# A conditioned feed-forward with routed low-rank experts: the chosen heads of two tiles turned by copies and VectorE instead of by TensorE, and deltas that follow later

## The chip, the cores and the metric

The kernel runs on one core of one Trainium2 chip. The metric is the device time of one execution in microseconds, as the median of several runs. A profile is one further execution, taken with the hardware profiler; its own time is given beside its span, because durations come from it.

## What is computed

The inputs are x (8 batches of 512 tokens, 2048 columns, float32), a base matrix W (2048 x 2048) with a bias, 32 low-rank adapters of rank 16 of which each batch uses one (`itok`), a router for 8 experts, and for each expert a projection A to 16 columns and a matrix B back to 2048. Cut to what matters:

```python
def cond(x, slot, W, b, As, Bs):                # x: (b t i)
    base = einsum('bti,oi->bto', x, W) + b
    return base + 2.0 * ((x @ As[slot]) @ Bs[slot])

def ffn(y, route_w, A, Bw):
    logits = einsum('bsd,ed->bse', y, route_w)  # 8 logits
    value, index = top_k(logits, 1)
    weight = one_hot(index, 8) * value
    h = einsum('bsd,erd->bser', y, A)           # 8 x 16 heads
    return einsum('bser,eor->bso', weight[..., None] * h, Bw)

out = x + ffn(cond(x, itok, ...), ...)
```

Nothing stands between the two parts but matrix products, so the kernel folds router and A (136 columns: 128 heads and 8 scores) into W and the adapters once for each batch, and multiplies x by the 2048 x 136 result.

## The kernel before

**Stages.** First W is read in 16 row blocks and folded with the projection (`fold_w`, L293), together with the adapters of the first batch. Then a loop runs over 32 tiles of 128 tokens. A pair of tiles is a unit; x is kept in five buffers of one unit each. `Q` is 32, `NQ` is 4.

**One tile.** The heads are `x_tile @ m`, with x turned so that its columns lie on partitions. The turn has two steps: `shuffle` (L249) copies 16 blocks of 32 partitions for a whole unit, some on ScalarE and some on GpSimd, so that each block of 32 x 32 lies where its transpose belongs; `turn_x` (L234) transposes blocks of 32 x 32 on VectorE (DVE). TensorE then multiplies 16 column blocks into a PSUM tile `ph` of 128 x 136 (`heads`, L452). `route` (L463 to L473) is the choice, six DVE instructions: add the constant part, take the greatest score, find its first place, and set all heads but the chosen 16 to zero, scaled by the score (`wh`). `turn_heads` (L520) transposes `wh` on TensorE into PSUM (`pw`), and `keep_heads` (L525) copies the result to SBUF on ScalarE (`whT`). `delta` (L558) multiplies `whT` by the experts' B (`fb`) in halves of 1024 columns (two matmuls of 512) into PSUM (`po`). `add_delta` (L571) adds such a half to x on DVE, and behind the second half `store` (L580) writes the tile out from the SP queue.

**Order.** The order of all engines is written out by hand (`manual_schedule`); each engine runs its instructions in the order in which the code issues them. The loop at L606 counts half tiles, n. In one n TensorE has 8 matmuls of heads, then a half delta. The half delta of n is that of half tile n - 3 (`piece`), its addition comes one n later, and the transposed heads stand at the end of even n. ScalarE and GpSimd have 4 shuffles in each n, for the unit that TensorE reaches some six n later.

**Folding an adapter.** For each batch but the first, `fold_adapter` (L481) makes the batch's matrix m in the n that `folded` lists (5, 11, 19, 27, 35, 43, 51): small products on TensorE (L349), copies on ScalarE (L504, L510), additions on DVE (L508), and three n later additions on GpSimd (`add_c`, L512). It uses both `po` buffers, so that n has no delta and the next n has two.

**PSUM.** There are 8 banks: `ps_s` and `ps_h` two tiles of one bank each, `ps_o` two tiles of two banks. `ph` of tile 0 lies in `ps_s`, that of the others in `ps_h`; `pw` and two products of a fold lie in `ps_s`.

**Loads.** `load_x` (L118) reads a unit into the buffer of the unit five before it, from the SP queue. It is issued five n behind the delta of that older unit's last half (L643), and has to wait until that unit is copied away and stored.

**The end.** For the last two tiles `ends` lists PSUM banks piece by piece; each piece of 512 or 256 columns is added and stored by itself, some of the last tile's from ScalarE's queue.

Of the kernel before, what the change touches and what calls it, by code (L numbers as in the profile page):

```python
# [9 lines left out]
F32 = mybir.dt.float32  # L10
# [8 lines left out]
def kernel(  # L19
# [33 lines left out]
    P = 128  # L53
# [24 lines left out]
    small = ctx.enter_context(tc.tile_pool(name="small", bufs=2))  # L78
    wctx = ctx.enter_context(ExitStack())
    wpool = wctx.enter_context(tc.tile_pool(name="wpool", bufs=1))  # L80
    ps_s = ctx.enter_context(tc.tile_pool(name="ps_s", bufs=2, space=bass.MemoryType.PSUM))
    ps_c = wctx.enter_context(tc.tile_pool(name="ps_c", bufs=1, space=bass.MemoryType.PSUM))

    ctx.enter_context(tc.manual_schedule())
# [43 lines left out]

    nc.scalar.copy(warm_a[:, 1:2], warm_a[:, :1])
    load_pj(1, 3, nc.scalar)  # L130
    pm = ps_s.tile([P, P], F32, tag="s", name="pm")
    for _ in range(12):
        nc.tensor.matmul(pm, warm, warm, start=True, stop=True)

    own_i = const.tile([P, B], I32, name="own_i")
    nc.gpsimd.iota(own_i, pattern=[[-R, B]], base=0, channel_multiplier=1)
# [105 lines left out]
    def shuffle(u, ms, copy):  # L242

        if not ms:
            return
        if u not in xq_tiles:
            xq_tiles[u] = qpool.tile([P, TPU, NQ, DQ], F32, tag="q", name=f"xq_{u}")
        for g, i in ms:
            copy(xq_tiles[u][ts(i, Q), :, g, :], x_tiles[u][ts(g, Q), :, ts(i, DQ)])  # L249
# [71 lines left out]
            copy(bq[ts(i, Q), g].rearrange("p (c a) -> p c a", a=Q), src[:, :, i, :])  # L321

    def project_bias():
        pb = ps_s.tile([P, NP], F32, tag="s", name="pb")
        nc.tensor.matmul(pb, warm, bp, start=True, stop=True)
        nc.vector.tensor_copy(c0b, pb)

    pg = ps_s.tile([P, NP], F32, tag="s", name="pg")

    def project_adapters():  # L330

# [90 lines left out]
                turn_x(0, h)  # L422
    first_products()
    wctx.close()
    ps_h = ctx.enter_context(tc.tile_pool(name="ps_h", bufs=2, space=bass.MemoryType.PSUM))
    ps_o = ctx.enter_context(tc.tile_pool(name="ps_o", bufs=2, space=bass.MemoryType.PSUM))
    xpool2 = ctx.enter_context(tc.tile_pool(name="xpool2", bufs=1))
    ms[1] = [xpool2.tile([P, n, NP], F32, name=f"m1_{n}") for n in parts]
    xpools.update({k: xpool2 for k in range(3, XB)})


    ph_tiles = {}
    wh_tiles = {}
    pw_tiles = {}
    whT_tiles = {}
    po_tiles = {}

    def batch_of(t):
        return t // TPB

    def place_heads(t):
        if t not in ph_tiles:

            pool, tag = (ps_h, "h") if t else (ps_s, "s")
            ph_tiles[t] = pool.tile([P, 512], F32, tag=tag, name=f"ph_{t}")

    def heads(t, j0, j1):
        if j0 == 0:
            place_heads(t)
        m = ms[batch_of(t) % 2]  # L450
        for j in range(j0, j1):
            nc.tensor.matmul(  # L452
                ph_tiles[t][:, :NP],
                xT_tiles[t][:, j, :],
                place(m, (j,))[:, 0, :],
                start=(j == 0),
                stop=(j == NJ - 1),
            )

    def route(t):  # L460

        ph = ph_tiles[t][:, :NP]
        nc.vector.tensor_tensor(ph, ph, c0b, ALU.add)  # L463
        top = small.tile([P, 1], F32, tag="top", name=f"top_{t}")
        nc.vector.tensor_reduce(top, ph[:, ER:NP], AX.X, ALU.max)
        key = ph_tiles.pop(t)[:, NP : NP + E]
        nc.vector.scalar_tensor_tensor(key, ph[:, ER:NP], top, rank, ALU.is_equal, ALU.mult)
        win = small.tile([P, 1], F32, tag="win", name=f"win_{t}")
        nc.vector.tensor_reduce(win, key, AX.X, ALU.max)
        rw = small.tile([P, E], F32, tag="rw", name=f"rw_{t}")  # L470
        nc.vector.tensor_scalar(rw, key, win, top, ALU.is_equal, ALU.mult)  # L471
        wh = small.tile([P, ER], F32, tag="wh", name=f"wh_{t}")
        nc.vector.tensor_tensor(  # L473
            wh.rearrange("p (e r) -> p e r", r=R),
            ph[:, :ER].rearrange("p (e r) -> p e r", r=R),
            rw.unsqueeze(2).to_broadcast([P, E, R]),
            ALU.mult,
        )
        wh_tiles[t] = wh

    def fold_adapter(b, t):  # L481

        place_heads(t + 1)
        lasts = [
            ps_s.tile([P, 512], F32, tag="s", name=f"pa_{b}_{k}")[:, :NP] for k in range(2)
        ] + [ph_tiles[t + k][:, ds(NP + E, NP)] for k in range(2)]
        banks = []  # L490
        for k in range(2):
            po = ps_o.tile([P, HN, 512], F32, tag="o", name=f"po_{b}_{k}")
            banks += [
                po[:, n, : GRP * NP].rearrange("p (j e) -> p j e", e=NP) for n in range(HN)
            ]

        for q in reversed(range(NQ)):
            adapter_product(b, lasts[q], q, 3)
        for n in range(3):
# [12 lines left out]
    def add_c(b):  # L512
# [2 lines left out]
            nc.gpsimd.tensor_tensor(place(m, js), place(m, js), place(cs, js), ALU.add)  # L515
        nc.gpsimd.tensor_tensor(m[1], m[1], cs[1], ALU.add)

    def turn_heads(t):
        pw = ps_s.tile([P, P], F32, tag="s", name=f"pw_{t}")
        nc.tensor.transpose(pw, wh_tiles.pop(t), ident)  # L520
        pw_tiles[t] = pw

    def keep_heads(t):
        whT_tiles[t] = small.tile([P, P], F32, tag="whT", name=f"whT_{t}")
        nc.scalar.copy(whT_tiles[t], pw_tiles.pop(t))  # L525

    def bank(tag, n):

        pool, shape = {
            "h": (ps_h, [P, 512]), "s": (ps_s, [P, 512]), "o": (ps_o, [P, HN, 512])  # L530
        }[tag]
        b = pool.tile(shape, F32, tag=tag, name=f"pe_{tag}")
        return n, (b[:, 0, :] if tag == "o" else b)[:, :n]


    ends = {
        (NT - 2, 0): (("o", 512), ("o", 512)),
        (NT - 2, 1): (("h", 512), ("s", 512)),
        (NT - 1, 0): (("h", 512), ("o", 512)),
        (NT - 1, 1): (("o", 512), ("h", 256), ("s", 256)),  # L540
    }

    def delta(t, h, within=None):

        c0 = h * D // 2
        if (t, h) in ends:
            cuts = ends[t, h]
        else:
            po = ps_o.tile([P, HN, 512], F32, tag="o", name=f"po_{t}_{h}")
            cuts = [(512, po[:, k, :]) for k in range(HN)]  # L550
            po_tiles[t, h] = [(ds(c0, D // 2), po.rearrange("p n d -> p (n d)"))]
        c = c0
        for cut in cuts:
            if (t, h) in ends:
                cut = bank(*cut)
                po_tiles.setdefault((t, h), []).append((ds(c, cut[0]), cut[1]))
            n, part = cut
            nc.tensor.matmul(part, whT_tiles[t], fb[:, ds(c, n)], start=True, stop=True)  # L558
            c += n
            if within:  # L560
                within()
                within = None

    def add_delta(t, h, n=None):

        u, k = divmod(t, TPU)
        pieces = po_tiles[t, h]
        po_tiles[t, h] = pieces[n:] if n else []
        for m, (cols, part) in enumerate(pieces[:n]):
            xs = x_tiles[u][:, k, cols]  # L570
            nc.vector.tensor_tensor(xs, xs, part, ALU.add)  # L571
            if (t, h) in ends:
                store(t, cols, nc.scalar if t == NT - 1 and m % 2 else nc.sync)
            elif h == 1:
                store(t, ds(0, D))

    def store(t, cols, eng=nc.sync):
        u, k = divmod(t, TPU)
        b, r = divmod(t, TPB)
        eng.dma_start(out=out[b, ts(r, P), cols], in_=x_tiles[u][:, k, cols])  # L580

    def piece(n):

        return divmod(n - 3, 2) if 0 <= n - 3 < 2 * NT else (-1, -1)

    def shuffle_slot(n):

# [11 lines left out]
        shuffle(*shuffle_slot(n), nc.gpsimd.tensor_copy)  # L599


    folded = {8 * b + (3 if b else 5): b + 1 for b in range(B - 1)}
    folds = folded.get
    adds_c = {8 * b + (5 if b else 6): b + 1 for b in range(B - 1)}.get

    for n in range(2 * NT + 4):  # L606
        t, h = divmod(n, 2)
        if t < NT:
            heads(t, h * HJ, h * HJ + HJ // 2)
            if n == 3:  # L610

                turn_heads(0)
            heads(t, h * HJ + HJ // 2, (h + 1) * HJ)
        tp, hp = piece(n - 1)
        if tp >= 0 and not folds(n - 1):
            add_delta(tp, hp)
        turn_x(t + 1, h)
        if h == 1 and 0 < t <= NT:
            keep_heads(t - 1)
        if folds(n):  # L620
            fold_adapter(folds(n), t)
        if h == 1 and t < NT:
            route(t)
        u, ms_u = shuffle_slot(n)
        shuffle(u, ms_u, nc.gpsimd.tensor_copy if n == 2 else nc.scalar.copy)
        if adds_c(n):
            add_c(adds_c(n))
        if folds(n):
            pass
        elif n == 2 * NT:  # L630

            delta(*piece(n), lambda: turn_heads(t - 1))
        else:
            if folds(n - 1):
                delta(*piece(n - 1))
                add_delta(*piece(n - 1))
            if piece(n)[0] >= 0:
                delta(*piece(n))
            if n == 2 * NT - 1:
                add_delta(*piece(n), 1)  # L640
        if h == 0 and 1 < t < NT:
            turn_heads(t - 1)
        tq, hq = piece(n - 5)  # L643
        u, k = divmod(tq, TPU)
        if tq >= 0 and hq == 1 and k == TPU - 1 and u + XB < NU:
            load_x(u + XB)


# [46 lines left out]
```

## Time and profile before

| what | value |
|---|---|
| median of 3 runs | 319.52 us (319.36 to 319.61) |
| the profiled execution's own time | 319.83 us |
| its span (first to last instruction) | 318.1 us |
| granted TensorE clock | 0.998 |
| busy: TensorE, DVE, ScalarE, GpSimd | 312.0, 237.7, 188.0, 163.0 us |
| matmuls of the heads (L452), of the deltas in `po` (L558), of W (L293): busy | 129.8, 111.7, 59.9 us |
| transposes of `wh` on TensorE (L520) | 32 |
| moved by DMA | 88.5 MB, 278 GB/s in the mean |
| longest wait: ScalarE's copy `whT` for `pw` | 56.4 us in 25 waits |
| GpSimd's shuffles for x to land | 32.8 us in 7 waits |
| a store of 1 MB, issue to landing | 4.9 us median, 3.9 from 285 us on |

Busy time is the time in which an engine had at least one instruction at work. In the lists of groups each line has source line, engine, operation, tile written and tile read, shape, count, busy time, mean of one in ns, and the idle time before it with what ended it. The chain is followed back from the last instruction, at each step to what released it. `PEld` is the loading of weights, which lies beside the matmuls. A matmul in float32 appears as two records.

### The profile page before, as it was taken

To read this page: it belongs to the slowest core of one execution; us is meant where nothing else is said; L and a number is where in the kernel's file an instruction comes from. 1 tells how busy PE (TensorE), PEld (TensorE's weight loads), DVE (VectorE), ACT (ScalarE), POOL (GpSimd) and SP (SyncE) were. 2 spreads that over 40 slices of the span, in tenths; PEclk is the share of its full clock that TensorE was granted. 3 is DMA by queue.
4 is the path that set the end of the run, shared out by engine and by line. 5 is a ranking of instruction groups with operands and counts; after the bars stand their busy time and mean duration, and the time that the engine had idled before them with its cause. 6 is when DMAs were issued, how large, how long until landed. Compare 5 with 4: busy or idle time off the path is not lost.

```text
span 318.1 us, 5569 instructions
## 1 busy us (share of the span) xinstructions
PE 312.0 (98%) x2140; PEld 246.9 (78%) x2140; DVE 237.7 (75%) x422; ACT 188.0 (59%) x245; POOL 163.0 (51%) x167
## 2 busy tenths in 40 slices
PE   8999999999999999999999999999999999999994
PEld 7999999999777777786777767777777777677762
DVE  2231788947888798878887987887888888888864
ACT  3332466748697497659765965677587749760000
POOL 1012085989994949094819553935396276710000
PEclk9999999999999999999999999999999999999999
DMA  7999999989323494959495858767685859444337
GB/s 276 413 363 415 422 422 418 418 315 388 143 117 158 173 362 169 384 199 374 160 395 178 364 174 354 249 280 247 282 317 213 322 236 364 168 168 169 162 149 249
DMA packets 15307, 88.52 MB, mean 278 GB/s; under 512 B 1696, under 2 KB 4016, under 8 KB 4912
## 3 DMA queue, kind: packets, MB, share of 16 engines
q1 hardware_dynamic: 14112, 85.45, 68.6%
q0 software_dynamic: 320, 2.11, 1.6%
q10 hardware_dynamic: 848, 0.61, 0.6%
q8 instruction: 17, 0.28, 0.4%
q14 instruction: 10, 0.08, 0.1%
HBM read 54.60 MB, written 33.55 MB: 277 GB/s over the span
## 4 chain that ended last, share of the span: by engine, by line
PE 96%; DMA 2%; DVE 1%; DVEq 0%; issue 0%
PE ph L452 38%; PE po L558 32%; PE pc L293 19%; DMA w<-in_w_dram 2%; PE po L349 2%; PE pg L333 1%; PE pw L520 1%; PE pe_o L558 1%; PE ph L349 1%; PE pe_h L558 1%; DVE x L571 0%; PE pc L349 0%; PE pe_s L558 0%; DVE m L370 0%; DVE wv L279 0%; DVEq L691 0%
## 5 line engine op out<-in xcount | busy, mean ns | idle before, releaser
L249 POOL COPY xq<-x 32x1024 f32<-32x1024 f32 x121 | 126.0, 1041 | 77.8 <-DMA x<-in_x_dram 32.8
L249 ACT COPY xq<-x 32x1024 f32<-32x1024 f32 x135 | 140.9, 1043 | 15.3 <-DMA x<-in_x_dram 13.3
L452 PEld LDWEIGHTS ph<-m,xT 128*128 128x128 f32 x1024 | 124.8, 190 | 21.1 <-issue 15.8
L452 PE MATMUL ph<-m,xT 128*128 128x136 f32 x1024 | 129.8, 280 | 0.3 <-DVE m L370 0.3
L558 PE MATMUL po<-fb,whT 128*128 128x512 f32 x240 | 111.7, 592 | 0.0
L571 DVE TENSOR_TENSOR x<-x,po 128x1024 f32<-128x1024 f32 x60 | 72.9, 1217 | 28.5 <-PE po L558 28.3
L234 DVE STREAM_TRANSPOSE xT<-xq 128x1024 f32<-128x1024 f32 x64 | 78.8, 1235 | 2.0 <-POOL xq L249 1.4
L558 PEld LDWEIGHTS po<-fb,whT 128*128 128x128 f32 x240 | 41.7, 190 | 32.0 <-issue 31.8
L293 PE MATMUL pc<-pj,wv 128*128 128x136 f32 x512 | 59.9, 280 | 0.3 <-DVE wv L279 0.3
L293 PEld LDWEIGHTS pc<-pj,wv 128*128 128x128 f32 x512 | 59.5, 190 | 0.5 <-DVE wv L279 0.5
L525 ACT COPY whT<-pw 128x128 f32<-128x128 f32 x32 | 8.5, 265 | 56.5 <-PE pw L520 56.4
L279 ACT COPY wv<-w 128x1024 f32<-128x1024 f32 (+1 forms) x17 | 16.8, 996 | 30.2 <-DMA w<-in_w_dram 28.5
L279 DVE COPY wv<-w 128x1024 f32<-128x1024 f32 (+1 forms) x17 | 11.6, 685 | 25.5 <-DMA w<-in_w_dram 14.9
L515 POOL TENSOR_TENSOR m<-m,c 128x408 f32<-128x408 f32 x14 | 14.4, 1048 | 1.6 <-ACT m L510 1.1
L221 POOL COPY ad_q<-ad_ar 32x512 f32<-32x512 f32 x12 | 9.3, 773 | 9.6 <-DMA ad_ar<-in_cond_a_dram,arow_i 9.1
L508 DVE TENSOR_TENSOR m<-c,po 128x408 f32<-128x408 f32 x14 | 7.5, 576 | 5.2 <-PE po L349 5.2
L504 ACT COPY m<-ph 128x136 f32<-128x136 f32 x14 | 3.1, 275 | 13.8 <-PE pa L349 13.8
L463 DVE TENSOR_TENSOR ph<-ph,c0b 128x136 f32<-128x136 f32 x32 | 9.1, 283 | 1.8 <-PE ph L452 1.8
L520 PEld LDWEIGHTS pw<-ident,wh 128*128 128x128 f32 x32 | 4.5, 141 | 7.4 <-issue 6.9
L473 DVE TENSOR_TENSOR wh<-ph,rw 128x128 f32<-128x128 f32 x32 | 9.3, 291 | 1.1
L391 POOL DMA_DIRECT2D bias_o<-in_bias_dram x1 | 0.7, 735 | 18.3 <-DVE bias_o L390 18.3
L471 DVE TENSOR_SCALAR rw<-ph,win,top 128x8 f32<-128x8 f32 x32 | 9.1, 284 | 1.2
(70 smaller groups left out, 147.1 us busy)
## 6 DMA issues: line engine op xcount, KB each, us to landing
x<-in_x_dram SPq DMA_DIRECT2D x32, 1024.0 KB, 8.9
out_dram<-x SPq DMA_DIRECT2D x30, 1024.0 KB, 4.9
w<-in_w_dram SPq DMA_DIRECT2D x16, 1024.0 KB, 11.7
out_dram<-x SPq DMA_DIRECT2D x6, 256.0 KB, 2.7
fb<-in_ffn_b_dram SPq DMA_DIRECT2D x1, 1024.0 KB, 13.6
pj<-in_proj_dram SPq DMA_DIRECT2D x2, 272.0 KB, 11.9
out_dram<-x ACTq DMA_DIRECT2D x1, 256.0 KB, 2.4
pj<-in_proj_dram SPq DMA_DIRECT2D x1, 204.0 KB, 9.8
```

Source lines behind the costliest of these rows:

```text
L221: copy(dst[:, :NQ], src[:, ts(q, NQ)])
L234: nc.vector.transpose(dst[:, ts(h, HJ), :].rearrange("p j (g t) -> p g j t", t=Q), src.rearrange("p g (j a) -> p g j a", a=Q)[:, :, ts(h, ...
L249: copy(xq_tiles[u][ts(i, Q), :, g, :], x_tiles[u][ts(g, Q), :, ts(i, DQ)])
L279: copy(dst[:, ts(k, n)], wr[:, ds(h * HJ + k * n, n)])
L293: nc.tensor.matmul(pcs[z][:, n, :], wv_tiles[oc, j // HJ][:, j % HJ, :], pj[:, oc, :], start=(oc == 0 and n == 0), stop=(oc == NO - 1), sk ...
L349: nc.tensor.matmul(out, ad_q[ts(q, Q), b // 2, n, :], g4[ts(q, Q), b, :], start=start, stop=True, skip_group_check=not start, tile_positio ...
L452: nc.tensor.matmul(ph_tiles[t][:, :NP], xT_tiles[t][:, j, :], place(m, (j,))[:, 0, :], start=(j == 0), stop=(j == NJ - 1),)
L463: nc.vector.tensor_tensor(ph, ph, c0b, ALU.add)
L473: nc.vector.tensor_tensor(wh.rearrange("p (e r) -> p e r", r=R), ph[:, :ER].rearrange("p (e r) -> p e r", r=R), rw.unsqueeze(2).to_broadca ...
L515: nc.gpsimd.tensor_tensor(place(m, js), place(m, js), place(cs, js), ALU.add)
L558: nc.tensor.matmul(part, whT_tiles[t], fb[:, ds(c, n)], start=True, stop=True)
L571: nc.vector.tensor_tensor(xs, xs, part, ALU.add)
```

## The change

- `route` takes a list of tiles. For tiles 0 to 7, 30 and 31 it is called for one tile, from tile 8 to 29 for two at once, behind the second one's heads. It has eight DVE instructions instead of six, with the comparisons written as operations on broadcast operands; the key lies in SBUF and no longer in PSUM.
- For tiles 0 to 7 the transpose stays on TensorE. From tile 8 on `move_heads` copies 16 blocks of 32 partitions of `wh` into `wq`, 9 of them on GpSimd and 7 on ScalarE, behind the shuffles of the even n after the choice; `turn_moved` transposes blocks of 32 x 32 on DVE straight into `whT`, one n later, behind that n's `turn_x` and ahead of its choice.
- `due` replaces `piece`: a half delta follows 3 half tiles behind at first, and one more after each of the first three folds (up to 6). At those folds the n that follows has one delta instead of two. The last deltas are made three half tiles later than before.
- A load of x is issued two n behind the older unit's last half delta, which puts it directly behind that unit's second store on the SP queue; before, another unit's store stood between the two.
- PSUM: `ps_s` and `ps_h` are one tile of two banks each. `ph` is one tile for a unit, alternately in the one and the other. `pw` and the folds' products lie in spare columns of such tiles. `ends` lists other banks: the last tile's second half is 512 columns and 256 in one `po` tile and 256 in `ps_s`.

The core of the diff:

```diff
-    def route(t):
-        ph = ph_tiles[t][:, :NP]
-        nc.vector.tensor_tensor(ph, ph, c0b, ALU.add)
-        nc.vector.tensor_reduce(top, ph[:, ER:NP], AX.X, ALU.max)
-        key = ph_tiles.pop(t)[:, NP : NP + E]
-        nc.vector.scalar_tensor_tensor(key, ph[:, ER:NP], top, rank, ALU.is_equal, ALU.mult)
-        nc.vector.tensor_reduce(win, key, AX.X, ALU.max)
-        nc.vector.tensor_scalar(rw, key, win, top, ALU.is_equal, ALU.mult)
...
+    def route(ts_):
+        n = len(ts_)
+        u, k = divmod(ts_[0], TPU)
+        ph = ph_tiles[u][:, k : k + n, :NP]
+        nc.vector.tensor_tensor(ph, ph, c0b.unsqueeze(1).to_broadcast([P, n, NP]), ALU.add)
...
+        nc.vector.tensor_reduce(top, ph[:, :, ER:NP], AX.X, ALU.max)
+        nc.vector.tensor_tensor(key, ph[:, :, ER:NP], wide(top), ALU.is_equal)
+        nc.vector.tensor_tensor(key, key, rank.unsqueeze(1).to_broadcast([P, n, E]), ALU.mult)
+        nc.vector.tensor_reduce(win, key, AX.X, ALU.max)
+        nc.vector.tensor_tensor(key, key, wide(win), ALU.is_equal)
+        nc.vector.tensor_tensor(key, key, wide(top), ALU.mult)
...
+    NS = 8
+    groups = [(t,) for t in range(NS)]
+    groups += [(t, t + 1) for t in range(NS, NT - TPU, TPU)] + [(NT - 2,), (NT - 1,)]
...
+    def move_heads(g):
+        wh = wh_tiles.pop(g[0])
+        wq = small2.tile([P, TPU, P], F32, tag="wq", name=f"wq_{g[0]}")[:, : len(g), :]
+        for m, (q, i) in enumerate(moves):
+            copy = nc.scalar.copy if m % 2 and m > 2 else nc.gpsimd.tensor_copy
+            copy(wq[ts(i, Q), :, ts(q, Q)], wh[ts(q, Q), :, ts(i, Q)])
+        wq_tiles[g[0]] = wq
+
+    def turn_moved(g):
+        whT = new_whT(g)
+        nc.vector.transpose(
+            whT.rearrange("p k t -> p (k t)"),
+            wq_tiles.pop(g[0]).rearrange("p k a -> p (k a)"),
+        )
...
     ends = {
-        (NT - 2, 0): (("o", 512), ("o", 512)),
-        (NT - 2, 1): (("h", 512), ("s", 512)),
-        (NT - 1, 0): (("h", 512), ("o", 512)),
-        (NT - 1, 1): (("o", 512), ("h", 256), ("s", 256)),
+        (NT - 2, 0): (("s", 0, 512), ("s", 1, 512)),
+        (NT - 2, 1): (("h", 0, 512), ("h", 1, 512)),
+        (NT - 1, 0): (("o", 0, 512), ("o", 1, 512)),
+        (NT - 1, 1): (("o", 0, 512), ("o", 1, 256), ("s", 0, 256)),
     }
...
-    for n in range(2 * NT + 4):
+    lag, LAG = 3, 6
+    due = {}
+    done = 0
+    for n in range(2 * NT + LAG):
+        end = done if folds(n) else max(done, min(n - lag + 1, 2 * NT))
+        due[n] = [divmod(p, 2) for p in range(done, end)]
+        done = end
+        if folds(n):
+            lag = min(lag + 1, LAG)
+
+    for n in range(2 * NT + LAG + 1):
         t, h = divmod(n, 2)
...
-        tp, hp = piece(n - 1)
-        if tp >= 0 and not folds(n - 1):
-            add_delta(tp, hp)
+        for p in due.get(n - 1, ())[-1:]:
+            add_delta(*p)
         turn_x(t + 1, h)
-        if h == 1 and 0 < t <= NT:
+        if h == 1 and 0 < t <= NS:
             keep_heads(t - 1)
+        if h == 1 and t > NS and t - 1 in groups:
+            turn_moved(groups[t - 1])
         if folds(n):
             fold_adapter(folds(n), t)
-        if h == 1 and t < NT:
-            route(t)
+        if h == 1 and t in groups:
+            route(groups[t])
         u, ms_u = shuffle_slot(n)
         shuffle(u, ms_u, nc.gpsimd.tensor_copy if n == 2 else nc.scalar.copy)
+        if h == 0 and t > NS and t - 1 in groups:
+            move_heads(groups[t - 1])
...
-            if folds(n - 1):
-                delta(*piece(n - 1))
-                add_delta(*piece(n - 1))
-            if piece(n)[0] >= 0:
-                delta(*piece(n))
+        for p in due.get(n, ())[:-1]:
+            delta(*p)
+            add_delta(*p)
+        for p in due.get(n, ())[-1:]:
+            delta(*p)
...
-        tq, hq = piece(n - 5)
-        u, k = divmod(tq, TPU)
-        if tq >= 0 and hq == 1 and k == TPU - 1 and u + XB < NU:
-            load_x(u + XB)
+        for q, r in due.get(n - 2, ()):
+            u, k = divmod(q, TPU)
+            if r == 1 and k == TPU - 1 and u + XB < NU:
+                load_x(u + XB)
```

## The prediction

> **What bounds the kernel now.** I read the page first (busy time, then the chain that ended last), then the chain in order of time, then the tile `pw`, then the engines' own timelines around an adapter fold, and last the DMA traffic of the final 15 us in slices of half a microsecond. The page:
>
> ```profile
> span 318.1 us, 5569 instructions
> ...
> PE 312.0 (98%) x2140; PEld 246.9 (78%) x2140; DVE 237.7 (75%) x422; ACT 188.0 (59%) x245; POOL 163.0 (51%) x167
> ...
> PE 96%; DMA 2%; DVE 1%; DVEq 0%; issue 0%
> ```
>
> TensorE carries 96% of the chain. A busy PE alone proves little, since matmul ends are modelled; the chain in order of time proves it. It names for each stretch what held up the end (start, length, what):
>
> ```profile
> 297.44 0.11 PE pw L520
> 297.55 1.85 PE ph L452 x16
> 299.40 1.72 PE po L558 x4
> 301.12 1.85 PE ph L452 x16
> 302.97 1.72 PE po L558 x4
> 304.69 0.11 PE pw L520
> 304.80 1.85 PE ph L452 x16
> 306.65 1.72 PE pe_o L558 x4
> ```
>
> No gap: from 71.8 to 312.8 us this goes on, a tile every 7.25 us (304.69 - 297.44), of which 2 x (1.85 + 1.72) = 7.14 is heads and deltas and 0.11 the transpose at L520. I call a half of a tile, 3.57 us, a slot; it is one n of the loop.
>
> **The change, part by part.** *TensorE transposes.* 24 of 32 go (tiles 8 to 31): 24 x 0.11 = 2.6 us off an unbroken chain. That is the whole gross gain.
>
> *Deltas later.* The lag grows at the folds of slots 5, 11 and 19, so that three half deltas of 1.72 us move behind the last heads: nothing in TensorE's sum, but 5.2 us less work before the last heads and as much more after.
>
> *Choice.* Two single choices take 2 x 1.51 us of DVE (210.08 to 211.59 from first to last start and end). The pair has eight instructions; by the rows for 32x272 (437 ns), 128x8 (168 to 234) and the reduction (167) about 0.44 + 0.18 + 0.23 + 0.18 + 3 x 0.17 + 0.44 = 2.0, with gaps 2.2; bounds 1.5 (width is free) and 3.0 (nothing is shared). The ten single choices get two instructions more, about 0.3 us each. All of it lies beside TensorE: DVE does per fold period of eight slots 8 x 1.22 (L571) + 8 x 1.24 (L234) + 2 x 2.2 + 2 x 0.4 + 2 x 0.58 (L508) = 26.1 of 29.9 us.
>
> *Moves.* Per group 9 copies on GpSimd and 7 on ScalarE of 32 x 64 (32 x 32 for a single). No row has that size; GpSimd's nearest (form, count, busy and mean ns):
>
> ```profile
> L249 POOL COPY xq<-x 32x1024 f32<-32x1024 f32 x121 | 126.0, 1041 | 77.8 <-DMA x<-in_x_dram 32.8 <-DVE wh L473 23.8 <-DVE ph L463 7.6
> ...
> L221 POOL COPY ad_q<-ad_ar 32x512 f32<-32x512 f32 x12 | 9.3, 773 | 9.6 <-DMA ad_ar<-in_cond_a_dram,arow_i 9.1
> ...
> L223 POOL COPY ad_q<-ad_ar 32x128 f32<-32x128 f32 x2 | 0.8, 380 | 0.0
> ```
>
> From 0.065 (1041 by size) to 1.04 us (size is free). I take the line through the two strided rows, 0.25 + 1.02 ns an element = 0.32, since 32x128 is the nearest: 9 x 0.32 = 2.8 us. ScalarE likewise (32x512 616, 32x1024 1043): 0.24 each, 1.7 us; bounds 0.19 (its 128x1 row) and 0.27. The 24 copies of L525 (0.265) go. The turn of 128x256 on DVE is between 0.31 (a quarter of 1.235) and 1.235; I take 0.4.
>
> *Is a pair ready in time?* Count from slot n = 8b+4, behind a fold, the tightest place. The choice stands on DVE behind the fold's two adds and ends about 3.2 us in. ScalarE ends the fold's copies 1.0 us in (203.27; the slot began at 202.26), then has five shuffles (5.27 us) queued ahead of the moves: 1.0 + 5.3 + 1.7 = 8.0. GpSimd: 3.2 + 2.8 = 6.0. The turn ends at 8.4. The pair's first delta stands two slots on, behind the heads: 5.48 (a slot with two deltas) + 3.57 + 1.85 = 10.9. Spare: 2.5 us; 0.8 us at slot 19's fold, whose next slot has one delta only; even with every upper bound but the 1.04, about none is lost. Behind the moves GpSimd has two shuffles and `add_c`, ScalarE two shuffles: 10.1 us, and DVE wants them at 10.3 for a transpose that heads use two slots later. Between folds the choice ends 1.1 us in and the delta is at 9.0: more spare.
>
> *Loads of x.* On SP's queue a load now stands right behind the second store of the buffer that it overwrites and waits for it to land. Add 1.22 + store 3.9 (landing alone, 285 to 307 us) = 5.1 us from the slot's start; before, it is issued 3.57 + 1.7 = 5.3 from there (200.96 against 199.27), with a foreign 1 MB store in front. Same time, less in front: 2 MB instead of 3. Shuffles wait no longer than now. Two-bank score tiles are reused two units later, 14 us after their readers: no wait.
>
> [...] GpSimd's copies took 1026 to 1042 ns in all 108 cases after 69.5 us, and up to 1442 before, while DVE copied W from SBUF. [...]
>
> **The tail takes part of it back.** The page's view of stretches (PE, PEld, DVE, ACT, POOL busy, clock, DMA share, GB/s):
>
> ```profile
> 308.00:308.50 0.50, 0.50 (x2) 0.19 (x1) 0.47 (x2) 0.00 (x0) 0.00 (x0) 1.00 1.23 492
> ...
> 310.50:311.00 0.50, 0.50 (x3) 0.26 (x2) 0.43 (x1) 0.00 (x0) 0.00 (x0) 1.00 1.09 369
> 311.00:311.50 0.50, 0.50 (x3) 0.26 (x2) 0.40 (x1) 0.00 (x0) 0.00 (x0) 1.00 1.12 320
> 311.50:312.00 0.50, 0.50 (x2) 0.21 (x2) 0.33 (x2) 0.00 (x0) 0.00 (x0) 1.00 1.00 340
> ...
> 315.00:315.50 0.50, 0.00 (x0) 0.00 (x0) 0.00 (x0) 0.00 (x0) 0.00 (x0) 1.00 1.01 297
> ```
>
> The last seven 256 KB and two 128 KB stores (2.1 MB) keep the DMA engines full from 310 to 316.1 at about 340 GB/s, while 1 MB stores pass at about 420 (2.5 us). TensorE yields 256 KB per 0.86 us, 305 GB/s: hardly less than the stores can take, so a queue, once there, stays. Let T be the end of the last heads, now 306.65. Tile 29's 1 MB store goes out at 306.0, T - 0.7, long before the small ones; the last one lands at 314.2 + 2.9 = 317.1. After the change T = 306.65 - 23 x 0.11 - 5.2 = 299.0. Behind T: choice to T + 1.9, add and store of tile 28, adds of tile 29 to T + 6.4 (TensorE gives its second half at 5.2), store from then, data from T + 7.1 (0.7 on, as the 306.0 store shows) to 9.6. The small stores, first at T + 7.1, queue behind: 9.6 + 2.1 MB at 340 = 15.8, landing 1.0 later as now (316.1 to 317.1): T + 16.8 = 315.8. Without the queue it would be T + 12.6 + 2.9 = 314.5. So 1.3 of the 2.6 us come back as queue. Bounds: 370 GB/s, 0.5 us less; moves of tile 31 at 0.38 each and a slow turn on DVE ahead of tile 29's add, 0.8 more. Net gain 1.3 (0.5 to 1.9).
>
> [...]
>
> **Sum.** 319.83 (profiled execution: span 318.1 and 1.7 around it) - 1.3 = 318.5; the same off the median, 319.52, is 318.2.
>
> **Rivals.**
> *A. The queue does not form* (small stores pass at over 400 GB/s beside the big one): 319.52 - 2.6 = 316.9. For: 492 and 508 in single slices with 1 MB stores. Against: a DMA share of 1.0 at 340 for 6 us.
> *B. Nothing measurable*: tile 31's moves and turn delay the adds and the queue keeps 2.1 or more of 2.6; 319.0 and up to 319.5.
> *C. Slower: small GpSimd copies hardly get cheaper with size.* Place: `wq` on the way to a pair's first delta. Point: 9 copies in 10.9 - 3.2 - 0.4 = 7.3 us behind a fold, 7.5 elsewhere: from 0.82 us a copy TensorE waits for every pair. At 1.04: 9 x 0.22 = 2.0 us x 11 pairs = 22, giving 340. For: 773 for half of 1041's size. Against: 380 for 32x128.
>
> **How the numbers follow.** Forecast 0.63, A 0.14, B 0.15, C 0.08. About 0.2% (0.64 us) is what a measurement of this kernel can tell from no change. Forecast's range is 317.6 to 319.0; a twentieth of it is within 0.2%, as is most of B. Faster 0.75, same 0.17, slower 0.08. The range takes in A and most of B, and leaves out C: 316.8 to 319.3.
>
> **What would show it.** Right: `pw` at 8 transposes; the chain without gaps to the last heads near 299.0; a DMA share of 1.0 over the last 8 us; the last stores landing over 4 us after issue, not 2.9. ScalarE's 56 us of waiting for `pw` shrink to the first eight tiles. Wrong: TensorE waiting on `whT` or DVE at slots behind folds (C, or a DVE that falls behind), DVE waiting for `xq` with its adds late, or a DMA share under 0.9 at the end with the last landing near 314.5 (A).

## The result and the profile after

The changed kernel takes **349.81 us** (median of 6 runs, 348.26 to 350.68), the kernel before 319.56 beside it: a ratio of 1.094, 95% interval 1.0915 to 1.0965. The forecast was 318.2, so even the sign was wrong. The page of the profile after (execution of 350.17 us):

```profile
span 348.2 us, 5682 instructions
...
PE 319.5 (92%) x2116; PEld 252.4 (72%) x2116; DVE 246.7 (71%) x411; ACT 203.4 (58%) x312; POOL 189.0 (54%) x284
...
PEclk9999999897896999899999999999999999999998
...
PE 84%; DVE 10%; DMA 2%; ACT 1%; issue 1%; DVEq 0%
```

Two things are to be seen. TensorE has 24 transposes less and yet is busy 7.5 us longer (319.5 against 312.0), and the time in which it is not busy rose from 6.1 to 28.7 us. The row of the granted clock dips, all in the first half apart from the last slice, which lies behind the last matmul. DVE now holds 10% of the chain. TensorE's waits (engine, tile, line, what it waited for; us in total, times, longest):

```profile
PE ph L456 <- DVE wh L486: 15.7, 5, 5.2
PE pm L325 <- DVE g L341: 2.9, 1, 2.9
PE ph L456 <- ACT m L513: 1.1, 6, 0.2
```

The five waits of L456 are the first heads of tiles 1, 3, 5, 7 and 31, each for the choice of the tile before it. Those are just the second tiles of the units whose tiles are chosen singly. Both tiles lie in one PSUM tile of two banks, and in the trace the first matmul into its second bank starts only when the last reader of the first one (L486) has ended, 0.05 to 0.15 us behind it in these five. The second line is the same thing in the folding of W: `pb` and `pg` lie in one tile `pm`, so the product for the constant part waits for L341, which reads the other bank. So is the third: a fold's last products lie in spare columns of a score tile, and the next heads into that tile wait for ScalarE to copy them (L513), 0.2 us at each of six folds.

Where tiles are chosen in pairs, the chain is what was forecast. In order of time (start, length, what):

```profile
201.24 1.85 PE ph L456 x16
203.09 1.72 PE po L591 x4
204.81 1.85 PE ph L456 x16
206.66 1.72 PE po L591 x4
```

No gap and no transpose: 7.14 us a tile instead of 7.25. The loss lies before 150 us, with one more wait at tile 31.

A held choice is also longer than it should be: that of tile 0 takes 3.71 us (80.55 to 84.26) where one took 1.51 before. DVE's timeline at tile 0 (start, length):

```profile
81.09 0.17 DVE L481 TENSOR_TENSOR key<-ph,top 128x8 f32<-128x8 f32 x1
81.29 0.49 DVE L482 TENSOR_TENSOR key<-key,rank 128x8 f32<-128x8 f32 x1
81.82 0.16 DVE L483 TENSOR_REDUCE win<-key 128x1 f32<-128x8 f32 x1
82.02 0.84 DVE L484 TENSOR_TENSOR key<-key,win 128x8 f32<-128x8 f32 x1
82.89 1.04 DVE L485 TENSOR_TENSOR key<-key,top 128x8 f32<-128x8 f32 x1
```

and GpSimd's in the same microseconds, in short windows (each line is two copies of 1.03 us with 0.04 between them, and the second copy of a line is the first of the next):

```profile
80.74 2.10 POOL L249 COPY xq<-x 32x1024 f32<-32x1024 f32 x2
...
81.81 2.10 POOL L249 COPY xq<-x 32x1024 f32<-32x1024 f32 x2
...
82.88 2.10 POOL L249 COPY xq<-x 32x1024 f32<-32x1024 f32 x2
```

GpSimd's copies end at 81.77, 82.84 and 83.91; L482, L484 and L485 end 0.02 us behind them, at 81.79, 82.86 and 83.93. The same holds for all 20 instructions of these three lines that took over 0.25 us: each ends 0.02 to 0.03 us behind an instruction of GpSimd. The three have both operands in SBUF. L481, of the same shape but with one operand in PSUM, takes 0.17. When GpSimd is idle, as at 92.1 or 323.6 us, all of them take 0.17.

Three theories follow, which can hold together:
- **S, the shared tile.** TensorE waits because unlike things lie in one PSUM tile.
- **P, a wait for GpSimd (POOL in the profile).** An instruction of DVE with two SBUF operands waits until GpSimd's running instruction has ended; this lengthens each choice.
- **C, the clock.** After a long wait TensorE runs at a lower clock for a while, so each wait costs more than its own length. Its rival is a clock that falls by itself, without a wait.

### The profile page after: what moved, and what is told of

Same layout as the page of the kernel before. It is cut to its first block, busy times and chain, and to the rows that moved or that the text cites. A ratio compares the mean times of both kernels' runs of the same rounds, so it can differ in the third digit from the quotient of the medians.

```text
span 348.2 us, 5682 instructions
## 1 busy us (share of the span) xinstructions
PE 319.5 (92%) x2116; PEld 252.4 (72%) x2116; DVE 246.7 (71%) x411; ACT 203.4 (58%) x312; POOL 189.0 (54%) x284
## 4 chain that ended last, share of the span: by engine, by line
PE 84%; DVE 10%; DMA 2%; ACT 1%; issue 1%; DVEq 0%
PE ph L456 34%; PE po L591 28%; PE pc L293 17%; DMA w<-in_w_dram 2%; DVE key L485 1%; DVE xT L234 1%; DVE x L597 1%; DVE key L484 1%; ACT m L513 1%; PE pm L333 1%; DVE g L341 1%; DVE key L482 1%; PE ph L349 1%; DVE wh L486 1%; PE pe_o L591 0%
## 5 line engine op out<-in xcount | busy, mean ns | idle before, releaser
L456 PEld LDWEIGHTS ph<-m,xT 128*128 128x128 f32 x1024 | 132.0, 197 | 43.7 <-issue 28.3
L249 POOL COPY xq<-x 32x1024 f32<-32x1024 f32 x121 | 126.0, 1041 | 49.0 <-ACT whT L547 21.4
L456 PE MATMUL ph<-m,xT 128*128 128x136 f32 x1024 | 136.0, 288 | 17.1 <-DVE wh L486 15.7
L591 PE MATMUL po<-fb,whT 128*128 128x512 f32 x240 | 113.4, 599 | 0.0
L293 PEld LDWEIGHTS pc<-pj,wv 128*128 128x128 f32 x512 | 60.7, 193 | 1.0 <-DVE wv L279 1.0
L555 POOL COPY wq<-wh 32x64 f32<-32x64 f32 (+1 forms) x117 | 26.3, 225 | 55.2 <-DVE wh L486 50.9
L555 ACT COPY wq<-wh 32x64 f32<-32x64 f32 (+1 forms) x91 | 21.6, 238 | 22.9 <-DVE wh L486 21.6
L279 ACT COPY wv<-w 128x1024 f32<-128x1024 f32 (+1 forms) x17 | 16.8, 996 | 30.2 <-DMA w<-in_w_dram 28.7
L279 DVE COPY wv<-w 128x1024 f32<-128x1024 f32 (+1 forms) x17 | 11.7, 695 | 27.9 <-DMA w<-in_w_dram 17.7
L547 ACT COPY whT<-ph 128x128 f32<-128x128 f32 x8 | 2.1, 266 | 34.9 <-PE ph L537 16.2
L513 ACT COPY m<-ph 128x136 f32<-128x136 f32 x28 | 5.6, 286 | 22.8 <-PE ph L349 22.8
L469 DVE TENSOR_TENSOR ph<-ph,c0b 128x272 f32<-128x272 f32 (+1 forms) x21 | 7.7, 365 | 6.3 <-PE ph L456 6.3
L525 POOL TENSOR_TENSOR m<-m,c 128x544 f32<-128x544 f32 x7 | 9.4, 1338 | 0.0
```

The costliest lines, as they stand in the source:

```text
L279: copy(dst[:, ts(k, n)], wr[:, ds(h * HJ + k * n, n)])
L293: nc.tensor.matmul(pcs[z][:, n, :], wv_tiles[oc, j // HJ][:, j % HJ, :], pj[:, oc, :], start=(oc == 0 and n == 0), stop=(oc == NO - 1), sk ...
L456: nc.tensor.matmul(ph, xT_tiles[t][:, j, :], place(m, (j,))[:, 0, :], start=(j == 0), stop=(j == NJ - 1),)
L513: nc.scalar.copy(m[1][:, q, :], lasts[q])
L555: copy(wq[ts(i, Q), :, ts(q, Q)], wh[ts(q, Q), :, ts(i, Q)])
L591: nc.tensor.matmul(part, whT_tiles[t], fb[:, cols], start=True, stop=True)
```

## The experiments

Profiled spans, and TensorE's busy and other time in them; medians of the runs with the ratio to the kernel before, beside which each ran (319.55 to 319.61):

| kernel | median us | ratio, 95% interval | span | PE busy | PE not busy | clock |
|---|---|---|---|---|---|---|
| after | 349.81 | 1.094 (1.0915 to 1.0965) | 348.2 | 319.5 | 28.7 | 0.968 |
| `pb` elsewhere | 345.59 | 1.083 (1.0789 to 1.0871) | 343.8 | 317.1 | 26.7 | 0.977 |
| waits filled | 343.83 | 1.0729 (1.0681 to 1.0777) | 343.9 | 325.9 | 18.0 | 0.984 |
| key in PSUM | 335.76 | 1.0505 (1.0471 to 1.054) | 334.4 | 313.8 | 20.6 | 0.987 |
| one-bank tiles | 326.16 | 1.0205 (1.0188 to 1.0222) | 324.1 | 312.5 | 11.6 | 0.996 |
| the same, half copies | 322.69 | one run | 320.9 | 311.4 | 9.5 | 0.994 |
| one-bank tiles, old choice | 318.75 | 0.9973 (0.9961 to 0.9984) | 316.8 | 309.6 | 7.2 | 0.999 |
| the same, short tail | 318.61 | 0.9973 (0.9964 to 0.9982) | 316.9 | 310.1 | 6.8 | 0.999 |
| the same, turn between | 318.12 | 0.9959 (0.9945 to 0.9972) | 316.2 | 309.1 | 7.1 | 0.998 |

With the waits filled, 11.3 us of TensorE's busy time are the added matmuls (3.72 + 5.17 + 2.38).

**`pb` elsewhere.** One line of the changed kernel:

```diff
-        pb = pm[:, 1, :NP]
+        pb = pcs[NQ + 1][:, 2, :]
```

> The product for the constant part (L325) is written into an unused third of a bank that the folded W fills, instead of into the second bank of the warm-up tile; nothing else changes. Theory S (two things in one PSUM tile make TensorE wait): the wait of 2.9 to 3.1 us before L325 goes, the first heads move from 76.4 back to about 71.8 us, and the time falls by about 4.6 us, to 345.2 (344.5 to 346). Theory P (GpSimd's copying stretches the choice, and that alone is the loss): unchanged, 349.8, since no choice runs there. Theory C (TensorE's clock falls by itself in this stretch): unchanged within 0.5 us.

It changes the output as well, by a relative 0.104: L325 now starts a new sum in a bank in which sums over W are still going on. That the folded matrix is what differs is my reading; no run shows it. Instructions, shapes and order stay. Measured: 345.59, 4.2 us less. In TensorE's waits L325 is gone, but a shorter one stands in its place, because the new bank is shared too:

```profile
PE ph L456 <- DVE wh L486: 16.0, 5, 5.2
PE pc L293 <- DVE c0b L326: 1.5, 1, 1.5
```

The first heads start at 73.67 instead of 76.40. So S holds for this wait: 2.7 of the 4.2 us are gone by there. The rest comes behind tile 1's wait, where the clock is at 0.50 for 3.4 us (82.0 to 85.4) instead of 6.8; why it is shorter there is not shown. The clock speaks for C as well: 0.50 from 63.0 to 66.5 us in the changed kernel, from the end of the wait of L325 on, and 1.00 all through that stage here. A clock that falls by itself should have fallen here too.

**Key in PSUM.** P alone is taken away:

```diff
-        key = small.tile([P, TPU, E], F32, tag="key", ...)[:, :n, :]
+        key = ph_tiles[u][:, k : k + n, ds(2 * NP + P, E)]
...
-        nc.vector.tensor_tensor(key, key, wide(top), ALU.mult)
+        rw = small.tile([P, TPU, E], F32, tag="rw", ...)[:, :n, :]
+        nc.vector.tensor_tensor(rw, key, wide(top), ALU.mult)
```

> The key of the choice lies in spare columns of the score tile in PSUM until its last product, so that none of its small instructions reads two operands from SBUF; the number of instructions stays eight. Theory P (instructions with two SBUF operands are stretched from 0.17 us to as much as 1.26 while GpSimd copies): L482, L484, L485 fall to about 0.17 to 0.2 us each, the five held choices get shorter by about 2 us each, and the time falls to about 339 (336 to 343). Theory S: the waits for the choice of tiles 0, 2, 4, 6 and 30 stay, each at the undisturbed length of a choice, about 2.5 us, and the time stays above 333. If the stretch has another cause than two SBUF operands, the time stays at 349.8 and the three lines stay at 0.4 to 0.5 us.

Measured: 335.76, 14.05 us less: 0.2 below the range that P gave (336 to 343), and above the 333 of S. The groups of the singles and TensorE's waits:

```profile
L482 DVE TENSOR_TENSOR ph<-ph,rank 128x8 f32<-128x8 f32 x10 | 1.7, 174 | 0.3
L484 DVE TENSOR_TENSOR ph<-ph,win 128x8 f32<-128x8 f32 x10 | 1.7, 174 | 0.3
```

```profile
PE ph L456 <- DVE wh L487: 7.6, 5, 3.0
PE pm L325 <- DVE g L341: 3.4, 1, 3.4
```

The means were 408 and 520 ns in the changed kernel and are 174 now, with GpSimd as busy as before (188.4 us). The five waits are still there, at half their length. So P is real and S is real beside it: the 8.1 us taken from these waits and 5.7 of TensorE's busy time (319.5 to 313.8) make up the gain. Shorter waits brought less low clock: ahead of the last matmul it is at 0.50 for 6.8 us here, and for 20.5 in the changed kernel.

**One-bank tiles.** The shared tiles are taken away: every score tile, `pb`, `pg` and the last pieces get a one-bank tile of their own. The choice has to be made tile by tile then, since a pair's wide operands need two banks in one tile; so this is not S alone, there are 32 choices instead of 21.

```diff
-    ps_s = ctx.enter_context(tc.tile_pool(name="ps_s", bufs=1, ...))
+    ps_s = ctx.enter_context(tc.tile_pool(name="ps_s", bufs=2, ...))
...
-        pb = pm[:, 1, :NP]
+        pb = ps_s.tile([P, 512], F32, tag="s", name="pb")[:, :NP]
...
-            ph_tiles[u] = pool.tile([P, TPU, 512], F32, tag=tag, name=f"ph_{u}")
-        return ph_tiles[u][:, k, :]
+            ph_tiles[t] = pool.tile([P, 512], F32, tag=tag, name=f"ph_{t}")
+        return ph_tiles[t]
...
-        if h == 1 and t in groups:
-            route(groups[t])
+        if h == 1 and t < NT:
+            route(t)
```

> Each score tile, the constant part, the adapter projection and the last pieces have a PSUM tile of one bank of their own, and the choice is made tile by tile, with the same eight instructions and the key in SBUF; moves, turns, order and lag stay. Theory S: all waits of TensorE for the choice of the even single tiles go, the chain is TensorE without gaps from 71.8 us on, and the time is 318.2 (317 to 319.5), what the prediction gave without these waits. Theory P as the cause by itself: the choices are stretched as before, there are now 22 of them more, and the time stays above 340. Theory C: the granted clock is back above 0.99 as soon as TensorE has nothing to wait for; if the clock falls by itself it stays near 0.97 and the time above 325.

Measured: 326.16, 23.65 us less: 8 above what S expected by itself, and far below the 340 of P by itself. No heads wait for a choice any more (two transposes do, 2.4 us in all), and the granted clock is back at 0.996, as C expected. The chain shows what is left:

```profile
81.50 0.92 DVE key L479
82.63 0.85 DVE key L481
83.51 1.05 DVE key L482
84.79 1.21 DVE x L598
86.00 1.16 DVE xT L234
87.16 1.10 DVE x L598
88.26 1.15 DVE xT L234
```

DVE itself has become the bound from 76 to about 185 us (32% of the chain), and the late store and load of x that follow from it hold the chain up to 203 us. With 32 choices, three stretched instructions in each (means 381, 504 and 328 ns against 166), it is 22.9 us busier than with short ones (32 x 0.715). My sentence "the choice lies beside TensorE" fails here a second time, without any shared tile.

**One-bank tiles, old choice.** Both are taken away; the choice is that of the kernel before, six instructions, key in PSUM:

```diff
-        nc.vector.tensor_tensor(key, ph[:, ER:NP], top.to_broadcast([P, E]), ALU.is_equal)
-        nc.vector.tensor_tensor(key, key, rank, ALU.mult)
+        key = place_heads(t)[:, ds(2 * NP + P, E)]
+        nc.vector.scalar_tensor_tensor(key, ph[:, ER:NP], top, rank, ALU.is_equal, ALU.mult)
...
-        nc.vector.tensor_tensor(key, key, win.to_broadcast([P, E]), ALU.is_equal)
-        nc.vector.tensor_tensor(key, key, top.to_broadcast([P, E]), ALU.mult)
+        nc.vector.tensor_scalar(rw, key, win, top, ALU.is_equal, ALU.mult)
```

> As e3_one_bank, but the choice is the one of before: six instructions, the key in PSUM, so that no instruction reads two SBUF operands. Theory S: the choice lies beside TensorE in both, so the time is that of e3_one_bank within 0.4 us, about 318. Theory P: the stretched choice costs even where TensorE does not share a tile with it, and this kernel is faster than e3_one_bank by 1 us or more. In either case its small instructions should stay at 0.17 to 0.25 us beside GpSimd's copies, against 0.3 to 0.5 in e3_one_bank.

Measured: 318.75, 0.8 below the kernel before and 7.4 below one-bank tiles. S alone had foretold the same time for both; P is needed. The chain behind an adapter fold, with moved and turned pairs:

```profile
166.13 2.12 PE ph L455 x16
168.25 3.43 PE po L590 x8
171.68 1.85 PE ph L455 x16
173.54 1.72 PE po L590 x4
```

No gap from 71.6 us to the last heads, which end at 299.13; the forecast had 299.0.

**Half copies.** Is it a wait for the end of an instruction, or shared bandwidth? One-bank tiles with each of GpSimd's shuffles cut in two:

```diff
-            copy(xq_tiles[u][ts(i, Q), :, g, :], x_tiles[u][ts(g, Q), :, ts(i, DQ)])
+            for ks in ((0, 1), (1, 2)) if copy == nc.gpsimd.tensor_copy else ((0, TPU),):
+                copy(
+                    xq_tiles[u][ts(i, Q), slice(*ks), g, :],
+                    x_tiles[u][ts(g, Q), slice(*ks), ts(i, DQ)],
+                )
```

> As e3_one_bank, but each of GpSimd's shuffles is two copies of 32x512 (773 ns in the profile before) instead of one of 32x1024 (1041). Theory P, in the form that an instruction of VectorE with two SBUF operands waits until GpSimd's running copy has ended: the longest of L479, L481 and L482's counterparts fall from 1.05 to about 0.8 us, those behind one another (second and third) from 0.94 to about 0.7, and with GpSimd idle all stay at 0.17; GpSimd's own busy time rises by about 60 us, and the time may go either way (322 to 332). If the stretch is a share of bandwidth and not a wait for the copy's end, the lengths stay as in e3_one_bank, up to 1.05 us. Nothing of the computation is changed.

A half copy takes 615 ns, less than the 773 I had taken from another form, so GpSimd is only 17 us busier (205.8). DVE's timeline, second and third instruction of two choices:

```profile
97.16 0.43 DVE L485 TENSOR_TENSOR key<-key,win 128x8 f32<-128x8 f32 x1
97.63 0.52 DVE L486 TENSOR_TENSOR key<-key,top 128x8 f32<-128x8 f32 x1
...
104.04 0.27 DVE L485 TENSOR_TENSOR key<-key,win 128x8 f32<-128x8 f32 x1
104.34 0.61 DVE L486 TENSOR_TENSOR key<-key,top 128x8 f32<-128x8 f32 x1
```

Beside copies the longest of the 39 cases is 0.61 us, where it was 1.04 with whole copies. The expectation that the longest of all falls to 0.8 failed: beside `add_c`, whose additions take 1.05 and 1.33 us on GpSimd, these instructions still take up to 1.25. That fits the same rule, since those were not cut. With GpSimd idle all 43 cases take 0.17. All instructions of this kind over 0.25 us, 35 with whole copies and 40 with half ones, end 0.015 to 0.03 us behind an instruction of GpSimd. So its running instruction sets the length, and not a share of bandwidth. The time, 322.69, 3.5 below one-bank tiles, is of a single run.

**Waits filled.** For C: the changed kernel with matmuls nobody reads in three of the waits.

```diff
+            for _ in range({2: 16, 6: 22, 14: 10}.get(n, 0)):
+                spare = place_heads(t + 1)[:, ds(NP + P + NP, 512 - NP - P - NP)]
+                nc.tensor.matmul(spare, warm, warm[:, : spare.shape[1]], start=True, stop=True)
             heads(t, h * HJ, h * HJ + HJ // 2)
```

> The changed kernel with 16, 22 and 10 idle matmuls (128x112, into unread columns of the next unit's score tile) ahead of the heads of tiles 1, 3 and 7, where TensorE waits 3.8, 5.2 and 3.2 us for the choice; the waits themselves are not shortened. Theory C (TensorE's clock is lowered because it has waited more than some 3 us): the granted clock behind these three waits stays near 1.00 instead of 0.50, 0.58 and 0.65, the 24 and 16 matmul records behind them take about 2.8, 1.9 and 1.9 us instead of 5.8, 4.0 and 3.1, and the time falls by about 6 to 8 us, to 342 to 344. If the clock falls for another reason (the program's place, power of the other engines), the clock stays at 0.5 to 0.65 there and the time at 349.8, or above by what the added matmuls overrun the waits.

The view of stretches (PE, PEld, DVE, ACT, POOL busy, clock, DMA share, GB/s), first of the changed kernel in tile 1's wait and behind it, then with it filled (1.7 us later, since in this profile the clock was low for 6.8 us in the folding of W instead of 3.4):

```profile
80.50:84.30 3.80, 0.01 (x1) 0.00 (x0) 3.51 (x9) 1.70 (x2) 3.63 (x5) 0.90 1.01 427
84.30:90.10 5.80, 5.79 (x25) 5.79 (x26) 2.24 (x2) 0.00 (x0) 4.83 (x5) 0.50 0.36 153
```

```profile
82.10:86.00 3.90, 3.69 (x34) 3.51 (x32) 3.49 (x9) 1.81 (x2) 3.73 (x5) 1.00 1.00 422
86.00:89.00 3.00, 2.97 (x25) 2.97 (x26) 2.25 (x2) 0.00 (x0) 2.88 (x4) 1.00 0.71 300
```

And TensorE's timeline, heads of tiles 1 and 5 (in brackets the idle time before), of the changed kernel and of this one:

```profile
84.31 5.81 PE L456 MATMUL ph<-m,xT 128*128 128x136 f32 x24 [3.80 <-DVE wh L486]
...
125.31 2.09 PE L456 MATMUL ph<-m,xT 128*128 128x136 f32 x16 [2.52 <-DVE wh L486]
```

```profile
86.03 3.05 PE L456 MATMUL ph<-m,xT 128*128 128x136 f32 x24 [0.24 <-DVE wh L486]
...
121.35 3.57 PE L456 MATMUL ph<-m,xT 128*128 128x136 f32 x16 [2.52 <-DVE wh L486]
```

The same 24 records take 5.81 us behind an idle wait and 3.05 behind a filled one; the clock stays at 1.00 instead of 0.50. The time fell by 6.0 us, to 343.83, as C expected, although nothing waits less long: from the last heads of a tile to the first of the next it is still 3.80 us at tile 1, 5.20 at tile 3 and 3.24 at tile 7. Tile 5's wait, which was not filled, was followed by full speed in one profile and by 3.57 us for 16 records in the other. The four runs went from 340.99 (clock 0.998) to 345.68 (0.984). The one at 0.998 lies 8.8 us below the changed kernel: if its waits are those of the profiled run, about that is what the low clock costs on top of them.

**Short tail, and turn between.** Two attempts at a better version, both on top of one-bank tiles with the old choice. The first puts the last two tiles' transposes back on TensorE and makes four half deltas at once ahead of the last heads; the second puts tile 31's transpose between two matmuls.

```diff
+        if n == 2 * NT - 2:
+            lag = 3
...
-        if h == 0 and 1 < t <= NS:
+        if h == 0 and (1 < t <= NS or NT - TPU < t <= NT):
             turn_heads(t - 1)
```

> As e4_old_choice, but the last two tiles are transposed on TensorE as before the change, and the deltas of tiles 28 and 29 are made at once behind tile 31's first heads, so that only four half deltas follow the last heads instead of six; the last pieces lie in one-bank tiles. If the part of the gain that the forecast gave up to the queue of stores (1.3 us) is really lost there, the span falls from 316.8 to about 315.5 and the time to 317.3 (316.9 to 317.8): 2.6 us of transposes less the two put back (0.2). If the stores are not what ends it, the time is that of e4_old_choice, 318.75, or 0.2 above.

Measured: 318.61, the same as before it within the interval: the hoped-for 317.3 was missed by 1.3 us, and of the two branches the one without a gain came true. The stores land sooner (2.7 us median instead of 4.4), but TensorE stood still for ScalarE's copy of tile 31 (0.28 us and the steps around it). So the second:

```diff
-            delta(*p)
-        if h == 0 and (1 < t <= NS or NT - TPU < t <= NT):
+            delta(*p, (lambda: turn_heads(NT - 1)) if n == 2 * NT else None)
+        if h == 0 and (1 < t <= NS or t == NT - 1):
```

> As e5_short_tail, but tile 31's transpose stands between the two matmuls of tile 30's last half instead of behind both, so that ScalarE's copy of it (0.28 us) lies beside a matmul. The trace of e5_short_tail shows TensorE without work for about 0.35 us at 308.2 for that copy, ahead of the last six pieces. If TensorE's end sets the end of the stores there, the time falls by 0.4 us against e5_short_tail, to 318.2 (317.9 to 318.4), 1.3 below the kernel before; if the drain of the stores sets it, it stays at 318.6.

Measured: 318.12, as expected, 1.5 below the kernel before (319.61 beside it): the fastest version here by its median. Its interval overlaps that of the short tail; the spans of the runs do not (316.0 to 316.3, against 316.5 to 316.9). Its last stretch:

```profile
306.22 0.86 PE pe_o L590 x2
307.08 0.11 PE ph L531
307.19 0.86 PE pe_o L590 x2
308.05 1.72 PE pe_h L590 x4
```

## Why the prediction was wrong

The step that failed is the sentence **"Two-bank score tiles are reused two units later, 14 us after their readers: no wait."** I looked at when a tile is used again and not at what happens inside it: its second bank is written while its first one is read. With it fell "All of it lies beside TensorE", and with that the place where the choice's cost counts. The runs put in its place:

- *Shared tiles (S).* TensorE waits 18.6 us (15.7 and 2.9) for readers of the other bank. Undone, together with the pairs' joint choice: 349.81 to 326.16.
- *Stretched choices (P).* Undone alone: 349.81 to 335.76. Both undone: 318.75. The parts (23.65 and 14.05) add up to more than the whole (31.06), since a shorter choice is worth most where TensorE waits for it.
- *Clock (C).* The same work keeps TensorE busy 319.5 us in the changed kernel and 309.6 with both undone. These 9.9 us of the 31.4 between the two spans are slower matmuls and not waiting; the other 21.5 are time in which it is not busy. Of the 9.9, about 8.9 are the low clock, by an estimate: TensorE is busy for 17.8 us of the 20.5 at 0.50, and I take that work to need half as long at 1.00 (the 24 records of tile 1 took 5.81 us at 0.50 and 3.05 at 1.00). With both undone the clock does not fall before the last matmul.

Step by step:
- *TensorE transposes*: right. 24 x 0.11 us are gone, and the last heads end at 299.13 (forecast 299.0) once nothing waits.
- *Choice*: the pair was sized rightly, 2.13 us by its rows (0.429 + 0.174 + 0.174 + 0.354 + 0.170 + 0.235 + 0.175 + 0.424) against 2.0. The singles were not: "about 0.3 us" more was forecast, and the three instructions alone add up to 1.47 us in the mean (0.408 + 0.520 + 0.537) and 2.37 at tile 0.
- *Moves and turn*: right, with GpSimd's copies sized too long. The groups of the changed kernel:

```profile
L555 POOL COPY wq<-wh 32x64 f32<-32x64 f32 x99 | 22.7, 229 | 44.3 <-DVE wh L486 40.6
L555 ACT COPY wq<-wh 32x64 f32<-32x64 f32 x77 | 18.6, 242 | 11.4 <-DVE wh L486 10.2
L560 DVE STREAM_TRANSPOSE whT<-wq 128x256 f32<-128x256 f32 x11 | 4.6, 422 | 1.7 <-ACT wq L555 1.6
```

  0.229, 0.242 and 0.422 us against 0.32, 0.24 and 0.4.
- *Is a pair ready in time*: right. No matmul's wait for a moved pair's `whT` is in the list.
- *Loads of x*: right in the direction; they land after 6.9 us in the median, where it was 8.9 before.
- *DVE beside GpSimd*: looked at from the wrong side. The prediction has the length of GpSimd's copies (1026 to 1042 ns after 69.5 us) and no wait of DVE in its sum. It is DVE that waits, up to 1.25 us an instruction, while GpSimd's copies still take 1041 ns in the mean. The trace of before could not tell, since in its loop no instruction of DVE has two SBUF operands. The runs tell: DVE's ends lie 0.02 to 0.03 us behind GpSimd's in all 20 long cases of the changed kernel, and with half copies the longest beside copies is 0.61 us instead of 1.04.
- *The tail*: right in its size. Of 2.6 us the queue of stores was to take 1.3; with both causes undone the span is 316.8, that is 318.1 - 1.3, the DMA share stays at 0.93 to 1.07 from 307 to 314 us, and the small stores land after 4.4 us. In the changed kernel too 17.7 us pass from the end of the last heads (330.5) to the end, where the forecast had 17.8. Two things it did not have: one addition of DVE waits 1.03 us there, by the trace for a store to land (309.47), and its cost was not tested; and with the tail shortened (turn between) the span fell by 0.6 us more, to 316.2, and not by 1.1 (the 1.3 less 0.2 for the two transposes put back).
- *Rivals*: A and B were not what happened. C, the slower one, was refuted at its place: 0.229 us a copy where it needed 0.82. The true slower mechanism was none of them.

So the sum was right for a kernel without the shared tiles and the stretched key, and wrong for this one. Left open: where between 326.16 and the forecast the shared tiles alone would lie with the choice still in pairs; how much of the gain of one-bank tiles comes from each of its three moves (score tiles, `pb`, last pieces), of which only `pb` was run alone; and a version with pairs in two banks and singles in one was not tried.

## What to carry to other kernels

When a change puts two things into one tile, ask who waits for whom inside the tile, not only when the tile is used again (TensorE waited 18.6 us here); in a new layout look up the first write into each part and the last read of its neighbour. A short instruction of DVE beside a busy GpSimd was not short here if both its operands lay in SBUF: one operand in PSUM, or GpSimd's work in smaller pieces, took it from 1.04 us to 0.17, or to at most 0.61 beside the copies. A gap in TensorE's work can cost more than its length (24 records took 5.81 us behind an idle wait of 3.80 and 3.05 behind a filled one), and filling it with work that nobody reads can win part of that back (6.0 us of 349.81).

## What the runs showed of the hardware

- The clock behind a wait: 0.50 for 5.8 us behind 3.80 us of idle TensorE, and 1.00 where matmuls that nobody reads filled it. Each low stretch ahead of the last matmul lasts 3.4 or 6.8 us. In the changed kernel the waits of 3.80, 5.20 and 3.24 us ahead of tiles 1, 3 and 7 were followed by one, and shorter waits were too: 2.89 us in the folding of W (0.50 from 63.0 to 66.5 us), 2.52 ahead of tile 5 in one of three profiles, and 1.95 ahead of tile 1 with the key in PSUM (0.50 from 83.2 to 86.6). Gaps of up to 1.55 us were not, nor was one of 3.39 in the folding of W with the key in PSUM. So the length alone does not decide, and a threshold of some 3 us is not shown.
- DVE and GpSimd: an instruction of DVE on 128x8 with both operands in SBUF takes 0.17 us alone and up to 1.25 beside GpSimd, as long as the rest of GpSimd's running instruction (its end is 0.02 to 0.03 us behind GpSimd's in all 20 cases over 0.25 us of the changed kernel). At tile 0 one such instruction gets in between two copies, and the next takes as long as a whole one, 1.04 us. GpSimd's copies of 32x1024 take 1041 ns in the mean before and after the change.
- Small copies across partitions in the changed kernel: 32x64 takes 229 ns and 32x32 202 on GpSimd, 242 and 215 on ScalarE.
